# Attention scores in stages of three head pairs instead of two, the third in the two projection banks

## The chip, the cores and the metric

The kernel runs on one core of one Trainium2 chip. The metric is the device time of one execution in microseconds; less is better. Every tensor is fp32.

## The reference

A decoder layer on x (4 batches, 1024 tokens, 512 features) with a context of 384 features per token. Three residual blocks follow each other:

```
x = x + attn(layernorm(x))          # 16 heads of 32; gated
x = x + xattn(layernorm(x), ctx)    # 16 heads of 32; keys and values from ctx
x = x + ffn(layernorm(x))           # 64 small networks of 16 hidden units

attn:  s = softmax(q k^T / sqrt(32)) * aperture * expression, divided by its row sum + 1e-8
       out = rotate(s v) @ Wout
xattn: out = softmax(q k^T / sqrt(32)) v @ Wo + bo
```

What matters here is the inner part of both attentions: for each batch, head and 1024 x 1024 pair of tokens a score, its exponential, the sum of exponentials over the keys, and the product with the values.

## The kernel before

The work is eight units: `ph` 0 (attn) for batches 0 to 3, then `ph` 1 (xattn) for batches 0 to 3. Each unit has two halves `hf` of 512 queries. A half has four groups `g` of four heads (HG = 4), and each group eight key tiles `kt` of 128 keys. One (g, kt) is a **step**; there are 8 x 2 x 4 x 8 = 512.

In a step, `scores(g, kt)` (L600) makes two **pairs**, i = 0 and 1, each of two heads. A pair gets a tile `s` of two PSUM banks (pool `ps`, two such tiles, L71). For each of its heads j, two matmuls of 32 rows x 64 columns fill the bank (L607 to L611): the head's 32 features lie on partitions (2i+j) x 32 onward, so that pair 0 uses array rows 0 to 63 and pair 1 rows 64 to 127. One ScalarE instruction exponentiates both banks into a tile `e` (L613; pool `p4`, six buffers, L612). VectorE adds the exponentials up over kt into `es` (L619, L621), for both pairs or for pair 0 alone where pair 1's sums are made on TensorE (`shared`, which is phase 0 and the last unit); in phase 0 it also adds them up weighted by a gate, `eg` (L629).

`times` (L632) multiplies a step's exponentials with the values: four column matmuls of 128 rows x 32 columns into the accumulator `av` (L635), and in shared units, every second step, four more into `sm` (L643). `step` (L718) puts them one step late: scores of step n, then `times` of step n-1. After the last key tile `normalize` (L649) has ScalarE copy `av` and `sm` away; `add_up` (L662) and `divide` (L686) come steps later through `after` (L346) and its `tick`, and move the sums through DRAM on the SP queue.

PSUM has eight banks: four for `s`, two for `bank()` (pool `pf`, L72, L80), one each for `av` and `sm`. `bank()` serves everything else: the projections of the next unit (q, k, v), the output projections, transposes and the feed-forward.

The projections are made by `columns` (L83), four column matmuls per chunk of the contraction. Each of a projection's three or four chunks is one part with its own load (`proj` L445, `values` L514, `project` L787). `run` (L967) issues a half's 32 steps and, after each, as many parts of the side work (`beside`, L1001) as fit the share of the load that is due. So a projection is cut between steps, at one to three chunks a step. After a projection's last chunk its bank is copied to SBUF (`evacuate` L277, on ScalarE once the first unit has begun; on VectorE for the values of phase 0, L537).

In this way TensorE's queue in a half reads: scores of a step, `av` of the step before, perhaps `sm`, one to three projection chunks, then the next scores. The order of every engine is the program's own; no scheduler changes it.

Of the kernel before, what the change touches and what calls it, by code (L numbers as in the profile page):

```python
# [10 lines left out]
F32 = mybir.dt.float32  # L11
# [52 lines left out]
def moderate_path(tc: tile.TileContext, a: dict, out: bass.AP, flag: bass.AP):  # L64
    nc = tc.nc
    x = a["x"]
    with ExitStack() as st:
# [9 lines left out]
        p3 = enter(tc.tile_pool(name="mp3", bufs=3))  # L77
        p4 = enter(tc.tile_pool(name="mp4", bufs=4))

        def bank():  # L80
            return pf.tile([P, HALF], F32, tag="f", name="f")

        def columns(to, lhsT, rhs, **flags):  # L83

# [272 lines left out]
        def pre(u):  # L357
# [87 lines left out]
            def proj(what, g, hf):  # L445
                kind = "ctx" if ph == 1 and what == "k" else "in"
                n = NCK if kind == "ctx" else NC

                def part(cs):
                    def f():  # L450
                        if cs[0] == 0:
                            if "w" + what not in me:
                                fetch(what)
                            me["pj"] = bank()
                        for c in cs:
# [58 lines left out]
            def values(kt):  # L514
# [5 lines left out]
                def part(cs):  # L520
                    def f():
                        if cs[0] == 0:
                            if kt == 0:
                                if "wv" not in me:
                                    fetch("v")
                                me["v"] = p2.tile([P, NT, H, DH], F32, tag="v", name="v")
                            me["pv"] = bank()
                        for c in cs:
# [56 lines left out]
        def attention(u, hf):  # L585
# [11 lines left out]
            def closing(g):  # L597
                return (u, hf, g) == (len(order) - 1, 1, HG - 1)

            def scores(g, kt):  # L600
                q, k = me["q", hf], me["k"]
                es = []
                for i in range(2):
                    s = ps.tile([P, 2, HALF], F32, tag="s", name="s")
                    for j in range(2):
                        r = slice((2 * i + j) * DH, (2 * i + j + 1) * DH)
                        for m in range(0, P, 64):  # L607
                            nc.tensor.matmul(  # L608
                                s[m : m + 64, j, :], lhsT=k[r, g, kt * P + m : kt * P + m + 64], rhs=q[r, g, :],
                                start=True, stop=True,  # L610
                            )  # L611
                    e = p4.tile([P, 2, HALF], F32, tag="e", name="e", bufs=6)  # L612
                    nc.scalar.activation(e, s, AF.Exp, scale=SCALE)  # L613
                    es.append(e)
                me["e", kt] = es
                for i in range(1 if shared and not closing(g) else 2):
                    if kt == 1:
                        me.setdefault("es", {})[i] = p1.tile([P, 2, HALF], F32, tag=f"es{i}", name="es")
                        nc.vector.tensor_tensor(me["es"][i], me["e", 0][i], es[i], ALU.add)  # L619
                    elif kt > 1:  # L620
                        nc.vector.tensor_tensor(me["es"][i], me["es"][i], es[i], ALU.add)  # L621
                if ph == 0 and kt > 0:
                    if kt == 1:
                        me["eg"] = p1.tile([P, 2, HALF], F32, tag="es1", name="eg")
                    for h in range(2):
                        eg, gate = me["eg"][:, h, :], lambda t: me["sw"][:, t, HG * g + h, 1:2]
                        if kt == 1:
                            nc.vector.tensor_scalar(eg, me["e", 0][0][:, h, :], gate(0), None, ALU.mult)
                        nc.vector.scalar_tensor_tensor(eg, es[0][:, h, :], gate(kt), eg, ALU.mult, ALU.add)  # L629
                return es  # L630

            def times(g, kt, es):  # L632
                for h in range(HG):
# [5 lines left out]
                if shared and kt % 2 and not closing(g):  # L639

                    for j in range(4):
                        t, h = kt - 1 + j // 2, j % 2
                        nc.tensor.matmul(  # L643
                            sm[j * DH : j * DH + sums, :],
                            lhsT=me["sw"][:, t, HG * g + 2 + h, :] if ph == 0 else ones, rhs=me["e", t][1][:, h, :],
                            start=(kt == 1), stop=(kt == NT - 1),
                        )

            def normalize(g):  # L649
                i = (u * 2 + hf) * HG + g  # L650
                both = p1.tile([P, 3, HALF], F32, tag="both", name="both")
                nc.scalar.copy(both[:, 0, :], av)
                if shared:
                    nc.scalar.copy(both[:, 1, :], sm)
                    added = [me["es"][0][:, 0, :], me["es"][0][:, 1, :]]
                    if ph == 0:
                        added += [me["eg"][:, 0, :], me["eg"][:, 1, :]]
                else:
                    added = [me["es"][h // 2][:, h % 2, :] for h in range(HG)]
                after(1, lambda: add_up(g, i, both, added), behind=True)  # L660

            def add_up(g, i, both, added):  # L662
# [52 lines left out]
                nc.vector.tensor_tensor(me["q", hf][:, g, :], both[:, 0, :], all_, ALU.mult)  # L715
                me["divided", hf] = g

            def step(g, kt):  # L718
                def f():
                    issue_due(False)  # L720
                    es = scores(g, kt)
                    issue_due(True)
                    if late:
                        late.pop(0)()
                    late.append(lambda: finish(g, kt, es))
                    tick[0] += 1
                return f

            def finish(g, kt, es):
                times(g, kt, es)  # L730
                if kt == NT - 1 and not closing(g):
                    normalize(g)

            for g in range(HG):
                for kt in range(NT):
                    steps.append(step(g, kt))
            return steps

        def settle(u, hf, g):

# [4 lines left out]
            def sums():  # L745
                for j in range(HG):
                    nc.tensor.matmul(
                        sm[j * DH : (j + 1) * DH, :], lhsT=ones.to_broadcast([P, DH]), rhs=me["es"][j // 2][:, j % 2, :],
                        start=True, stop=True,
                    )  # L750

# [10 lines left out]
        def post(u, hf):  # L762
# [24 lines left out]
            def project(t):  # L787
                def part(cs, to=None):
                    def f():
                        assert last or me["divided", hf] >= cs[-1]  # L790
                        if cs[0] == 0:
                            res["po"] = to() if to else bank()
                            res["po", t] = res["po"]
                        if last:
                            res["po"] = res["po", t]
                        for c in cs:
# [167 lines left out]
                done = upto  # L964
            return [out + second[done:]]

        def run(main, items):  # L967

            parts = sum(items, [])
            total = sum(c for c, _ in parts)  # L970
            done = 0
            for n, f in enumerate(main):
                f()
                while parts and (done + parts[0][0] / 2 <= total * (n + 1) / len(main) or n == len(main) - 1):
# [26 lines left out]
        def beside(u, hf):  # L1001
# [77 lines left out]
        run([lambda: None], first)  # L1079
# [7 lines left out]
        late.pop(0)()  # L1087

        def go(*parts):
            for _, f in parts:  # L1090
# [673 lines left out]
```

## Time and profile before

| | |
|---|---|
| median of three runs | 2196.32 us (2192.43 to 2196.33) |
| profiled execution | 2195.77 us |
| its span | 2193.9 us, 53076 instructions |
| TensorE's granted clock, mean | 0.997 |
| L87, all projections: largest row (f<-xT,w) | 333.7 us busy, 2816 records, 592 ns |
| L621, es additions on VectorE | 642.4 us busy, 534 of 1227 ns |
| L629, eg additions on VectorE | 318.4 us busy, 448 of 746 ns |
| L652, L654, L666, copies of av and sm on ScalarE | 37.3, 23.9 and 37.4 us busy, 591 to 613 ns |
| mean DMA rate | 74 GB/s |

How to read it: PE is TensorE's matmuls, PEld its weight loads, which run beside them. DVE is VectorE, ACT ScalarE, POOL GpSimd, SP the engine whose queue issues most transfers. A group's line gives the line of code, engine, operation, out<-in with shapes, the count, busy time and mean duration in ns, then the engine's idle time before the group and what ended it. Ends of matmuls are modelled, and a matmul's 592 ns overlap with the next ones; what TensorE really spends is read from the distance between starts. An fp32 matmul leaves two records.

### The profile page before, as it was taken

To read this page: it belongs to the slowest core of one execution; us is meant where nothing else is said; L and a number is where in the kernel's file an instruction comes from. 1 tells how busy PE (TensorE), PEld (TensorE's weight loads), DVE (VectorE), ACT (ScalarE), POOL (GpSimd) and SP (SyncE) were. 2 spreads that over 40 slices of the span, in tenths; PEclk is the share of its full clock that TensorE was granted. 3 is DMA by queue.
4 is the path that set the end of the run, shared out by engine and by line. 5 is a ranking of instruction groups with operands and counts; after the bars stand their busy time and mean duration, and the time that the engine had idled before them with its cause. 6 is when DMAs were issued, how large, how long until landed. Compare 5 with 4: busy or idle time off the path is not lost.

```text
span 2193.9 us, 53076 instructions
## 1 busy us (share of the span) xinstructions
PE 2168.4 (99%) x22750; PEld 557.5 (25%) x22750; DVE 1558.3 (71%) x2510; ACT 1240.3 (57%) x1493; POOL 85.3 (4%) x127
## 2 busy tenths in 40 slices
PE   9999999999999999999999999999999999999996
PEld 4322222222222222222222222222222222222223
DVE  4578675796757957577686676877777777856477
ACT  0155545555455554555656566675757666577673
POOL 2000000030300000000000000000000000000000
PEclk9999999999999999999999999999999999999998
DMA  6312133032330221211222132221223142203131
GB/s 170 117 47 72 56 97 105 19 89 66 101 113 19 85 66 51 84 37 42 69 85 94 41 93 65 79 82 48 68 89 108 50 103 69 81 20 85 54 89 41
DMA packets 154137, 161.72 MB, mean 74 GB/s; under 512 B 47002, under 2 KB 92698, under 8 KB 152740
## 3 DMA queue, kind: packets, MB, share of 16 engines
q1 hardware_dynamic: 149828, 156.14, 24.7%
q8 instruction: 180, 2.95, 0.6%
q0 software_dynamic: 2080, 0.98, 0.3%
q10 hardware_dynamic: 1984, 1.12, 0.2%
q14 instruction: 65, 0.53, 0.1%
HBM read 115.40 MB, written 42.74 MB: 72 GB/s over the span
## 4 chain that ended last, share of the span: by engine, by line
PE 94%; DVE 2%; ACT 1%; issue 1%; DMA 1%; SPq 0%; POOL 0%; DVEq 0%; ACTq 0%
PE f L87 36%; PE s L608 25%; PE av L635 21%; PE sm L643 6%; PE sm L665 3%; ACT e L613 1%; DVE es L621 1%; PE f L913 1%; PE f L875 1%; PE s L87 1%; DVE g L902 1%; DMA xin<-in_x 0%; PE f L483 0%; PE s L913 0%; ACT hid L896 0%
## 5 line engine op out<-in xcount | busy, mean ns | idle before, releaser
L613 ACT ACTIVATE e<-s 128x1024 f32<-128x1024 f32 x1024 | 993.7, 1022 | 709.5 <-PE s L608 511.9
L621 DVE TENSOR_TENSOR es<-es,e 128x1024 f32<-128x1024 f32 x534 | 642.4, 1227 | 266.0 <-ACT e L613 264.2
L608 PE MATMUL s<-q,k 32*64 32x512 f32 x8192 | 607.3, 613 | 2.4 <-ACT e L613 0.8
L635 PE MATMUL av<-e,v 128*32 128x512 f32 x4096 | 550.2, 603 | 0.0
L87 PE MATMUL f<-xT,w 128*32 128x512 f32 x2816 | 333.7, 592 | 0.0
L629 DVE SCALAR_TENSOR_TENSOR eg<-e,sw,eg 128x512 f32<-128x512 f32 x448 | 318.4, 746 | 2.3
L619 DVE TENSOR_TENSOR es<-e 128x1024 f32<-128x1024 f32 x89 | 106.7, 1223 | 220.3 <-ACT e L613 188.4
L608 PEld LDWEIGHTS s<-q,k 32*64 32x64 f32 x8192 | 132.8, 129 | 446.2 <-ACT e L613 241.8
L87 PE MATMUL f<-w,q 128*32 128x512 f32 x1984 | 240.3, 592 | 0.0
L635 PEld LDWEIGHTS av<-e,v 128*32 128x32 f32 x4096 | 87.9, 108 | 403.9 <-issue 401.3
L87 PEld LDWEIGHTS f<-xT,w 128*32 128x32 f32 x2816 | 92.1, 110 | 210.5 <-issue 206.0
L643 PE MATMUL sm<-e,sw 128*2 128x512 f32 x1024 | 133.3, 592 | 0.0
L87 PE MATMUL f<-w,xT 128*32 128x512 f32 x896 | 106.0, 592 | 0.6 <-DVE q L285 0.6
L87 PEld LDWEIGHTS f<-w,q 128*32 128x32 f32 x1984 | 65.5, 110 | 149.1 <-issue 142.6
L87 PE MATMUL f<-w,ctxT 128*32 128x512 f32 x768 | 92.6, 592 | 0.0
L896 ACT ACTIVATE hid<-sT,units 128x256 f32<-128x256 f32 x128 | 76.5, 605 | 28.5 <-DVE g L902 24.1
L87 PE MATMUL f<-ctxT,w 128*32 128x512 f32 x768 | 92.3, 592 | 0.0
L812 POOL TENSOR_TENSOR r<-res,bo_bc 128x512 f32<-128x512 f32 x32 | 40.9, 1278 | 1041.5 <-DVE res L804 790.9
L902 DVE SCALAR_TENSOR_TENSOR g<-hid,units,g 128x256 f32<-128x256 f32 x120 | 57.5, 479 | 14.2 <-ACT hid L896 9.1
L665 PE MATMUL sm<-es,fixed 128*1 128x512 f32 x348 | 65.0, 591 | 0.0
L804 DVE TENSOR_TENSOR res<-f,res 128x512 f32<-128x512 f32 x62 | 42.5, 685 | 14.9 <-PE f L87 11.1
L715 DVE TENSOR_TENSOR q<-both,recb 128x512 f32<-128x512 f32 x63 | 43.2, 685 | 7.0 <-DMA recb<-rec_d 7.0
(265 smaller groups left out, 1046.2 us busy)
## 6 DMA issues: line engine op xcount, KB each, us to landing
recb<-rec_d SPq DMA_DIRECT2D x252, 64.0 KB
xT<-rows_d SPq DMA_DIRECT2D x60, 256.0 KB
rows_d<-r SPq DMA_DIRECT2D x60, 256.0 KB
w<-in_xattn_Wo SPq DMA_DIRECT2D x9, 1024.0 KB
w<-wout_d SPq DMA_DIRECT2D x8, 1024.0 KB
res<-in_x SPq DMA_DIRECT2D x32, 256.0 KB
x1b_d<-r SPq DMA_DIRECT2D x32, 256.0 KB
res<-x1b_d SPq DMA_DIRECT2D x32, 256.0 KB
```

The source lines that it names most:

```text
L87: nc.tensor.matmul(to[r], lhsT=lhsT[:, j, :] if len(lhsT.shape) == 3 else lhsT[:, r], rhs=rhs, **flags)
L608: nc.tensor.matmul(s[m : m + 64, j, :], lhsT=k[r, g, kt * P + m : kt * P + m + 64], rhs=q[r, g, :], start=True, stop=True,)
L613: nc.scalar.activation(e, s, AF.Exp, scale=SCALE)
L619: nc.vector.tensor_tensor(me["es"][i], me["e", 0][i], es[i], ALU.add)
L621: nc.vector.tensor_tensor(me["es"][i], me["es"][i], es[i], ALU.add)
L629: nc.vector.scalar_tensor_tensor(eg, es[0][:, h, :], gate(kt), eg, ALU.mult, ALU.add)
L635: nc.tensor.matmul(av[r, :], lhsT=me["v"][:, kt, HG * g + h, :], rhs=es[h // 2][:, h % 2, :], start=(kt == 0), stop=(kt == NT - 1),)
L643: nc.tensor.matmul(sm[j * DH : j * DH + sums, :], lhsT=me["sw"][:, t, HG * g + 2 + h, :] if ph == 0 else ones, rhs=me["e", t][1][:, h, :], ...
L665: nc.tensor.matmul(sm[j * DH : j * DH + 1, :], lhsT=ones, rhs=e, start=True, stop=True)
L715: nc.vector.tensor_tensor(me["q", hf][:, g, :], both[:, 0, :], all_, ALU.mult)
L896: nc.scalar.activation(hid, res["s"], AF.Relu, bias=units[:, 1, h : h + 1], scale=units[:, 0, h : h + 1])
L902: nc.vector.scalar_tensor_tensor(res["g"], res["hid"], units[:, 2, h - 1 : h], res["g"], ALU.mult, ALU.add)
```

## The change

A half's 64 pairs (g, kt, i) are now listed in order, and a **phase** takes three at a time instead of a step taking two; the last of a half takes the one that is left. If a projection is open in a bank at that moment (`open_`, counted by `keep`), it takes two. The first two pairs of a phase get `s` tiles, the third two tiles of `bank()`. The third pair's exponentials are two ScalarE instructions of 512 columns, one for each bank. Where a projection is due right after and the phase has three pairs (`front`), the pairs are multiplied in the order 1, 2, 0, so that pair 0 lies in the banks; ScalarE still takes them in the order 0, 1, 2 and so empties the banks first.

`times` of the steps that the phase before completed come after the phase's scores; one or two steps, since three pairs complete one step and a half. Where a group ends (`border`), the first of them, which ends the group, comes after the first exponential, and the other after the side work of the phase. `tick` now advances by 1.5.

`run_phases` takes the place of `run`: it issues side work after a phase's scores, and does not stop while a projection is open, so that each projection is issued whole. A projection is due by its first chunk's place in the load.

`e`, `es` and `eg` now share one tag with eight buffers (`wide`); before, `e` had six, and `es` and `eg` buffers of their own. In the last unit a pause in the side work is 14 or 12 instead of 10.

```diff
+        def keep(first, last):
+            open_[0] += bool(first) - bool(last)
...
+            def multiply_into(g, kt, i, two):
                 q, k = me["q", hf], me["k"]
-                    s = ps.tile([P, 2, HALF], F32, tag="s", name="s")
-                    e = p4.tile([P, 2, HALF], F32, tag="e", name="e", bufs=6)
-                    nc.scalar.activation(e, s, AF.Exp, scale=SCALE)
+                for j in range(2):
+                    r = slice((2 * i + j) * DH, (2 * i + j + 1) * DH)
+                    for m in range(0, P, 64):
+                        nc.tensor.matmul(
+                            two[j][m : m + 64], lhsT=k[r, g, kt * P + m : kt * P + m + 64], rhs=q[r, g, :],
+                            start=True, stop=True,
+                        )
+
+            def wide():
+                return p4.tile([P, 2, HALF], F32, tag="e", name="e", bufs=8)
+
+            def exponentials(g, kt, i, two, whole):
+                e = wide()
+                if whole is not None:
+                    nc.scalar.activation(e, whole, AF.Exp, scale=SCALE)
+                else:
                     for j in range(2):
+                        nc.scalar.activation(e[:, j, :], two[j], AF.Exp, scale=SCALE)
+                me.setdefault(("e", g, kt), {})[i] = e
...
-            def step(g, kt):
-                def f():
-                    issue_due(False)
-                    es = scores(g, kt)
-                    issue_due(True)
-                    if late:
-                        late.pop(0)()
-                    late.append(lambda: finish(g, kt, es))
-                    tick[0] += 1
-                return f
...
+            pairs = [(g, kt, i) for g in range(HG) for kt in range(NT) for i in range(2)]
+
+            def phase(size, early):
+
+                issue_due(False)
+                mine, pairs[:] = pairs[:size], pairs[size:]
+                front = early and size == 3
+                order_ = [1, 2, 0] if front else range(len(mine))
+                places = {}
+                for n, j in enumerate(order_):
+                    whole = ps.tile([P, 2, HALF], F32, tag="s", name="s") if n < 2 else None
+                    two = [bank(), bank()] if whole is None else [whole[:, m, :] for m in range(2)]
+                    multiply_into(*mine[j], two)
+                    places[j] = (two, whole)
+                border = len(late) > 1 and late[0][0] == NT - 1
+                for n, pair in enumerate(mine):
+                    exponentials(*pair, *places[n])
+                    add(*pair)
+                    if n == 0 and border:
+                        issue_due(True)
+                        late.pop(0)[1]()
+                issue_due(True)
+                while late and not border:
+                    late.pop(0)[1]()
+                now = list(late)
+                late.clear()
+                for g, kt, i in mine:
+                    if i == 1:
+                        late.append((kt, lambda g=g, kt=kt: finish(g, kt, me["e", g, kt])))
+                tick[0] += size / 2
+                return lambda: [f() for _, f in now]
...
+        def run_phases(pairs, phase, items):
...
+            while pairs:
+                size = min(len(pairs), 2 if open_[0] else 3)
+                upto = total * (all_ - len(pairs) + size) / all_
...
+                others = phase(size, early)
+                while parts and (open_[0] or due(parts[0][0], done)):
                     c, f1 = parts.pop(0)
                     if f1:
                         f1()
                     done += c
+                others()
...
-                out += pause(2) + weave(h[0:k], pause(10)) + weave(h[k:], last["o"]) + held.pop()["out"]
+                out += pause(2) + weave(h[0:k], pause(14 if hf else 12)) + weave(h[k:], last["o"]) + held.pop()["out"]
...
-                run(attention(u, hf), beside(u, hf))
+                run_phases(*attention(u, hf), beside(u, hf))
```

More of the change, by code (lines that the diff above doesn't have):

```diff
@@ L78, in moderate_path @@
         p4 = enter(tc.tile_pool(name="mp4", bufs=4))
+        open_ = [0]
         def bank():
             return pf.tile([P, HALF], F32, tag="f", name="f")
+        def keep(first, last):
+            open_[0] += bool(first) - bool(last)
         def columns(to, lhsT, rhs, **flags):
@@ L454, in f @@
                             me["pj"] = bank()
+                        keep(cs[0] == 0, cs[-1] == n - 1)
                         for c in cs:
@@ L527, in f @@
                             me["pv"] = bank()
+                        keep(cs[0] == 0, cs[-1] == n - 1)
                         for c in cs:
@@ L598, in closing @@
                 return (u, hf, g) == (len(order) - 1, 1, HG - 1)
-            def scores(g, kt):
+            def multiply_into(g, kt, i, two):
                 q, k = me["q", hf], me["k"]
-                es = []
-                for i in range(2):
-                    s = ps.tile([P, 2, HALF], F32, tag="s", name="s")
-                    for j in range(2):
[L606 to L611, printed above, removed]
-                    e = p4.tile([P, 2, HALF], F32, tag="e", name="e", bufs=6)
[L613 to L616, printed above, removed]
-                    if kt == 1:
[L618 to L622, printed above, removed]
@@ new lines, in add @@
+            def add(g, kt, i):
+                if kt == 0:
+                    return
+                e0, e = me["e", g, 0], me["e", g, kt]
+                if i == 0 or not shared or closing(g):
+                    if kt == 1:
+                        me.setdefault(("es", g), {})[i] = wide()
+                        nc.vector.tensor_tensor(me["es", g][i], e0[i], e[i], ALU.add)
+                    else:
+                        nc.vector.tensor_tensor(me["es", g][i], me["es", g][i], e[i], ALU.add)
+                if ph == 0 and i == 0:
@@ L623, in scores @@
                     if kt == 1:
-                        me["eg"] = p1.tile([P, 2, HALF], F32, tag="es1", name="eg")
+                        me["eg", g] = wide()
                     for h in range(2):
-                        eg, gate = me["eg"][:, h, :], lambda t: me["sw"][:, t, HG * g + h, 1:2]
+                        eg, gate = me["eg", g][:, h, :], lambda t: me["sw"][:, t, HG * g + h, 1:2]
                         if kt == 1:
-                            nc.vector.tensor_scalar(eg, me["e", 0][0][:, h, :], gate(0), None, ALU.mult)
@@ L629, in scores @@
-                        nc.vector.scalar_tensor_tensor(eg, es[0][:, h, :], gate(kt), eg, ALU.mult, ALU.add)
-                return es
+                            nc.vector.tensor_scalar(eg, e0[0][:, h, :], gate(0), None, ALU.mult)
+                        nc.vector.scalar_tensor_tensor(eg, e[0][:, h, :], gate(kt), eg, ALU.mult, ALU.add)
             def times(g, kt, es):
@@ L644, in times @@
                             sm[j * DH : j * DH + sums, :],
-                            lhsT=me["sw"][:, t, HG * g + 2 + h, :] if ph == 0 else ones, rhs=me["e", t][1][:, h, :],
+                            lhsT=me["sw"][:, t, HG * g + 2 + h, :] if ph == 0 else ones, rhs=me["e", g, t][1][:, h, :],
                             start=(kt == 1), stop=(kt == NT - 1),
@@ L654, in normalize @@
                     nc.scalar.copy(both[:, 1, :], sm)
-                    added = [me["es"][0][:, 0, :], me["es"][0][:, 1, :]]
+                    added = [me["es", g][0][:, 0, :], me["es", g][0][:, 1, :]]
                     if ph == 0:
-                        added += [me["eg"][:, 0, :], me["eg"][:, 1, :]]
+                        added += [me["eg", g][:, 0, :], me["eg", g][:, 1, :]]
                 else:
-                    added = [me["es"][h // 2][:, h % 2, :] for h in range(HG)]
+                    added = [me["es", g][h // 2][:, h % 2, :] for h in range(HG)]
                 after(1, lambda: add_up(g, i, both, added), behind=True)
@@ L732, in finish @@
                     normalize(g)
[L734 to L737, printed above, removed]
+            pairs = [(g, kt, i) for g in range(HG) for kt in range(NT) for i in range(2)]
[27 more added lines that the diff above has]
+                return lambda: [f() for _, f in now]
+            return pairs, phase
         def settle(u, hf, g):
@@ L747, in sums @@
                     nc.tensor.matmul(
-                        sm[j * DH : (j + 1) * DH, :], lhsT=ones.to_broadcast([P, DH]), rhs=me["es"][j // 2][:, j % 2, :],
+                        sm[j * DH : (j + 1) * DH, :], lhsT=ones.to_broadcast([P, DH]), rhs=me["es", g][j // 2][:, j % 2, :],
                         start=True, stop=True,
@@ L793, in f @@
                             res["po", t] = res["po"]
+                        keep(cs[0] == 0, cs[-1] == NC - 1)
                         if last:
@@ L965, in weave, with run, due @@
             return [out + second[done:]]
-        def run(main, items):
+        def run(items):
+            for _, f1 in sum(items, []):
+                if f1:
+                    f1()
+        def run_phases(pairs, phase, items):
             parts = sum(items, [])
-            total = sum(c for c, _ in parts)
+            total, all_ = sum(c for c, _ in parts), len(pairs)
             done = 0
-            for n, f in enumerate(main):
-                f()
-                while parts and (done + parts[0][0] / 2 <= total * (n + 1) / len(main) or n == len(main) - 1):
+            while pairs:
+                size = min(len(pairs), 2 if open_[0] else 3)
+                upto = total * (all_ - len(pairs) + size) / all_
+                def due(c, at):
+                    return at + min(c, 1) * 2 <= upto or len(pairs) == 0
+                early, at = False, done
+                for c, f1 in parts:
+                    if early or not due(c, at):
+                        break
+                    early, at = bool(c and f1), at + c
+                others = phase(size, early)
+                while parts and (open_[0] or due(parts[0][0], done)):
                     c, f1 = parts.pop(0)
@@ L1078, in moderate_path @@
         first += p["v"][1][0:3] + pres[1]["tr"][0] + p["v"][1][3:]
-        run([lambda: None], first)
+        run(first)
         for u in range(n):
@@ L1083, in moderate_path @@
             for hf in range(2):
-                run(attention(u, hf), beside(u, hf))
+                run_phases(*attention(u, hf), beside(u, hf))
         tail = ending[0]
         sums, divide, look = settle(n - 1, 1, HG - 1)
-        late.pop(0)()
+        late.pop(0)[1]()
         def go(*parts):
```

## The prediction

> **What bounds the kernel now.** I read the page's totals first, then its slices and the chain that ended last, then the costliest groups, and last the order of time around two score stages.
>
> ```profile
> PE 2168.4 (99%) x22750; PEld 557.5 (25%) x22750; DVE 1558.3 (71%) x2510; ACT 1240.3 (57%) x1493; POOL 85.3 (4%) x127
> ...
> PEclk9999999999999999999999999999999999999998
> ...
> PE 94%; DVE 2%; ACT 1%; issue 1%; DMA 1%; SPq 0%; POOL 0%; DVEq 0%; ACTq 0%
> PE f L87 36%; PE s L608 25%; PE av L635 21%; PE sm L643 6%; PE sm L665 3%; ACT e L613 1%; DVE es L621 1%; PE f L913 1%; PE f L875 1%; PE s L87 1%; DVE g L902 1%; DMA xin<-in_x 0%; PE f L483 0%; PE s L913 0%; ACT hid L896 0%
> ```
>
> TensorE is the bound: busy 99%, at the full granted clock, and 94% of the chain. So a change pays only where it takes time out of TensorE's own queue, and it costs whatever it puts in. A quarter of the chain is the scores of L608, the very thing that is regrouped.
>
> ```profile
> L613 ACT ACTIVATE e<-s 128x1024 f32<-128x1024 f32 x1024 | 993.7, 1022 | 709.5 <-PE s L608 511.9
> ...
> L608 PE MATMUL s<-q,k 32*64 32x512 f32 x8192 | 607.3, 613 | 2.4 <-ACT e L613 0.8
> L635 PE MATMUL av<-e,v 128*32 128x512 f32 x4096 | 550.2, 603 | 0.0
> ```
>
> A score matmul uses 32 rows and 64 columns of the array, the other work 128 rows and 32 columns; a matmul leaves two records, one for each fp32 pass. TensorE's idle time does not show as idle, because ends are modelled; so I read starts. First an ordinary stage of two pairs, TensorE alone:
>
> ```profile
> 802.58 0.61 PE L87 MATMUL f<-xT,w 128*32 128x512 f32 x4
> 803.12 1.11 PE L608 MATMUL s<-q,k 32*64 32x512 f32 x16
> 804.16 0.64 PE L635 MATMUL av<-e,v 128*32 128x512 f32 x4
> ```
>
> The stage takes 1.04 us from its first matmul to the next work's. Its 16 records start in two bursts of eight, 0.48 us apart: both pairs run side by side. Elsewhere one pass of four column matmuls follows the last after 0.43 us; into the stage it is 0.54, and the first pass after it takes 0.45. Now a stage whose second pair came late:
>
> ```profile
> 101.63 0.21 PEld L608 LDWEIGHTS s<-q,k 32*64 32x64 f32 x8 [1.03 <-ACT e L613]
> 101.63 2.00 PE L608 MATMUL s<-q,k 32*64 32x512 f32 x16
> 102.55 0.21 PEld L608 LDWEIGHTS s<-q,k 32*64 32x64 f32 x8 [0.71 <-ACT e L613]
> 102.79 1.94 ACT L613 ACTIVATE e<-s 128x1024 f32<-128x1024 f32 x2 [0.29 <-PE s L608]
> 103.56 0.16 PEld L635 LDWEIGHTS av<-e,v 128*32 128x32 f32 x8 [0.81 <-issue]
> 103.56 1.06 PE L635 MATMUL av<-e,v 128*32 128x512 f32 x8
> ```
>
> The two pairs run one behind the other, at 101.63 and 102.55, and the stage takes 1.93 us: a pair that cannot lie beside another costs 0.89 us more. That is the row the forecast rests on.
>
> Over all 512 stages in the trace, from first score to next work: 435 take 1.04 to 1.08 us, 22 take 1.88 to 1.94, the rest lie between; the sum is 571.7 us, 37 us above 512 x 1.044. Those 37 us are nearly all that TensorE waits for ScalarE today.
>
> **The change, part by part.** It is done as said: in the built order of TensorE the 512 stages of eight score matmuls become 336 of twelve and 16 of four (each half unit has 64 pairs, 21 x 3 + 1). Nothing else on TensorE changes in number.
>
> *Fewer switches: a gain.* A switch costs 0.54 - 0.43 on entry and 0.45 - 0.43 after, together 0.137 us unrounded. There are 512 - 352 = 160 fewer: -21.9 us. What the stage itself loses at its ends is in its length, next.
>
> *A third pair in a stage: the cost.* A pair i uses array rows 64i to 64i+63 (heads 2i and 2i+1, the slice in L606). Pairs come in turn i = 0, 1, 0, then 1, 0, 1, so the third is always on the rows of one of the others, and its two passes must follow that one's two. The other half of the array stands empty meanwhile. Nearest row: the serial stage, 1.93 us, +0.89. From below: two bare passes, 2 x 0.429 = +0.86. From above: +0.89 and what it waits for its banks (below). I take the row. 336 x 1.932 + 16 x 1.044 = 665.8 us for 571.7: +94.2 us. This assumes that all 37 us of late second pairs go; if all stay, it is +131.
>
> Two rules of the Trainium skill bear on this. TensorEngine Tiling (Array Packing), section Tiling Modes, says that changing the tiling mode drains the engine; that speaks for fewer stages, and the rows price it: 0.137 us outside the stage and 1.044 - 0.858 = 0.186 inside. TensorE: Matmul & The Clock Gate, Part 3, gives a pack's span as one matmul plus about 4 ns for each further tile. By that alone twelve matmuls would cost about 1.06 us: 336 x 1.06 + 16.7 - 571.7 - 21.9 = -221 us. But it counts distinct tiles, and the first page's list has eight tiles in the 32x64 mode, all of which the two pairs already fill. The rows agree with eight (16 records in two bursts, a late pair at full price), so I use +0.89.
>
> *The third pair's PSUM.* It takes the two projection banks, and is written last, 0.91 us into the stage. After a whole projection one of these banks must first be evacuated: a 128x512 ScalarE copy is 0.59 us (L281's row), and in the trace it starts about 0.1 us after the last matmul; some 0.85 us into the stage it is done, just inside the cover of the first two pairs. If ScalarE is busy then, the third pair waits and with it av, sm and everything queued behind on TensorE. VectorE evacuates some values (L537), behind 1.23 us additions: up to 1 us each, for some 24 projections. Below nothing: no, because the bank had no such reader before.
>
> *Exponentials by halves.* Two 128x512 ones replace a wide one 336 times. Wide ones start 0.92 us apart (1.94 us for two); halves by the copy row 0.59 each, about 0.5 apart: +0.06 to +0.26 us x 336 = 20 to 90 us of ScalarE, which is 57% busy. TensorE's projections hide it where a phase has one. In phases without one ScalarE needs 2 x 0.92 + 1.0 = 2.9 us for the three pairs from 1.15 us into the stage (804.27 - 803.12 in the ordinary stage), so the banks come free at about 2.2, 3.1 and 4.1. The next stage starts at 1.93 + 0.86 + 0.13 = 2.9 us with four av matmuls, 3.8 with av and sm or two steps of av, 4.6 with both. From the built order: 35 phases of the first kind, 29 of the second, some 30 of the third. The second pair and the third (due 0.91 later) are late by 0.3 to 1.3 us in the first, about 0.4 in the second, not in the third: 35 x 0.5 + 29 x 0.4 = 29 us; between 10 and 60. I take 28.
>
> *e, es and eg in one pool of eight.* Before, six e plus their own es. Now es and eg hold two of eight, four where one g passes to the next. By the built order's waits an exponential then waits for av of the same phase, issued right after the scores; ScalarE stalls under the projection, at no cost where there is one. It is in the 10 to 60.
>
> *Projections whole, evacuations, ticks.* Same matmuls in the same mode: nothing. The delayed steps now come due in ticks of 1.5, so sums, the reciprocal and the product with q come up to one step later. Their SP queue transfers (rec_d, recb, sums) move with them, past the loads and rows_d there; the output projections that need q lie later still, and SP moves 74 GB/s on average. Nothing; if that cover is gone, one late q costs a few us once in a half unit. VectorE's work stays 71% and the same.
>
> Sum: -21.9 + 94.2 + 28 = +100 us. Span 2193.9 + 100 = 2294; the profiled execution took 2195.77, so 1.9 lie around the span: 2296. The median of the runs, 2196.32, is 0.5 above that execution, nothing beside the rest.
>
> **The rivals.**
>
> *No new waits.* Three pairs give ScalarE slack, and with bare passes the third pair costs 0.86: 94.2 - 10 - 21.9 = +62 us, 2258. For it: ScalarE is 57% busy. Against: its slack is not in the phases without projections. 0.12.
>
> *ScalarE and the e buffers become the bound in phases.* Each of some 100 phases without a projection, and the borders between g, lose 1 to 1.5 us: +72 + 100 or more, 2350. For it: 22 stages are already serial today, many in the last unit. Against: the average phase has 2294 / 352 = 6.5 us for 3.5 us of ScalarE. 0.10.
>
> *The other side: the third pair is not serial.* If its passes slip under the others' second pass, at one pass only, a stage is 1.47 us: 336 x 1.474 + 16.7 - 571.7 - 21.9 = -82 us, with waits 2140. It decides at the stage's length: below 1.71 us the change gains (571.7 + 21.9 - 16.7 = 576.9, over 336), before waits. Against it: the same tiles must stream 512 columns twice, 0.43 us a pass wherever it is seen. 0.03.
>
> **How the numbers follow.** Main case 0.75, time 2296; its own width is the waits of 10 to 60 us, 2278 to 2328. I reach to the first rival and a little above the main case: 2258 to 2335. Left out: most of the second rival, and the third. Slower 0.97, faster 0.02, within 0.2% 0.01; 0.2% (4 us) is about what a measurement can tell.
>
> **What would show it.** Right: 352 stages, ordinary ones of twelve taking 1.9 us or more, with a third burst 0.91 us after the first and a fourth; TensorE still 99% busy; the score line's share of the chain up from 25% to about 29%; ScalarE's wide exponentials down to 688. Wrong: twelve matmuls in under 1.7 us; or stages often over 2.3 us, with TensorE's wait for the exponentials as the long row; or TensorE well below 99%, which would make buffers or ScalarE the cause.

## The result, and the profile after

The changed kernel takes 2480.03 us (2471.74 to 2486.74, 4 runs) against 2195.37 us (4 runs of it, one more than in the table of before): ratio 1.130, 95% interval 1.126 to 1.134. The direction was right, and the size was not: 285 us more where 100 were forecast, and 145 us above the end of the range. The profiled execution, which the account below is made from, is the fastest of the four: 2471.74 us.

The page of the changed kernel, its totals, clock and chain:

```profile
span 2470.0 us, 53205 instructions
...
PE 2356.1 (95%) x22750; PEld 661.5 (27%) x22750; DVE 1560.7 (63%) x2510; ACT 1261.8 (51%) x1829; POOL 84.7 (3%) x127
...
PEclk9999999999999999999989999999999999999998
...
PE 57%; DVE 3%; ACT 3%; issue 1%; DMA 1%; SPq 0%; DVEq 0%; ACTq 0%
```

TensorE was 99% busy and 94% of the chain; now 95% and 57%. The forecast named this as a sign that it was wrong ("TensorE well below 99%, which would make buffers or ScalarE the cause"). The scores were to take about 29% of the chain, and take 19% (`s` and `f` of L612). The granted clock, 0.997 before, is 0.981 on average here and 0.974 to 0.980 in the other three runs. The groups of the page say who was waited for:

```profile
L623 ACT ACTIVATE e<-s 128x1024 f32<-128x1024 f32 x688 | 673.1, 1032 | 213.1 <-PE s L612 122.4
L626 ACT ACTIVATE e<-f 128x512 f32<-128x512 f32 x672 | 370.0, 599 | 532.7 <-PE f L612 400.2
...
L612 PE MATMUL f<-q,k 32*64 32x512 f32 x2688 | 417.3, 597 | 33.3 <-DVE v L544 10.1
...
L659 PE MATMUL sm<-e,sw 128*2 128x512 f32 x1024 | 135.5, 601 | 33.7 <-ACT both L682 33.7
```

The third pairs' matmuls (`f` of L612) wait for VectorE's copy of a projection, and the `sm` matmuls for ScalarE's copy of a finished group's sums. Neither group had such a wait before: the scores of L608 had 2.4 us in all, and the `sm` group none:

```profile
L643 PE MATMUL sm<-e,sw 128*2 128x512 f32 x1024 | 133.3, 592 | 0.0
```

First an ordinary stage of three pairs, TensorE alone, to see that the price of the third pair itself was right:

```profile
1719.92 0.61 PE L92 MATMUL f<-w,ctxT 128*32 128x512 f32 x4
1720.46 1.11 PE L612 MATMUL s<-q,k 32*64 32x512 f32 x16
1721.40 1.04 PE L612 MATMUL f<-q,k 32*64 32x512 f32 x8
1722.36 1.07 PE L651 MATMUL av<-e,v 128*32 128x512 f32 x8
```

The third pair starts 0.94 us in, and the stage takes 1.90 us; 203 of the 336 stages of three take 1.86 to 1.92. Now one stage with its surroundings, where the rest of the time is:

```profile
616.14 2.32 PE L612 MATMUL s<-q,k 32*64 32x512 f32 x16
...
618.28 1.02 PE L612 MATMUL f<-q,k 32*64 32x512 f32 x4
...
618.49 1.41 DVE L646 SCALAR_TENSOR_TENSOR e<-e,sw 128x512 f32<-128x512 f32 x2
619.82 0.54 DVE L309 TENSOR_SCALAR xin<-xin,bnmv,yi 128x512 f32<-128x512 f32 x1
620.27 0.69 DVE L544 TENSOR_TENSOR v<-f,sw 128x512 f32<-128x512 f32 x1
...
621.01 1.97 PE L612 MATMUL f<-q,k 32*64 32x512 f32 x4 [1.71 <-DVE v L544]
622.91 0.11 PEld L681 LDWEIGHTS sm<-e,fixed 128*1 128x1 f32 x8 [1.61 <-issue]
622.91 1.89 PE L681 MATMUL sm<-e,fixed 128*1 128x512 f32 x8
...
624.83 1.08 ACT L626 ACTIVATE e<-f 128x512 f32<-128x512 f32 x2 [7.51 <-PE sm L681]
625.80 1.95 ACT L623 ACTIVATE e<-s 128x1024 f32<-128x1024 f32 x2
...
627.61 0.62 ACT L682 COPY both<-sm 128x512 f32<-128x512 f32 x1
...
628.28 1.04 PE L659 MATMUL sm<-e,sw 128*2 128x512 f32 x8 [1.78 <-ACT both L682]
```

Three things follow each other. The third pair's first head starts at 618.28. The second head's bank still holds a value projection that ended before 616.14; VectorE gets to it at 620.27, behind its additions and a layernorm step, so the head starts at 621.01, 2.7 us after the first, where in the ordinary stage above both start together. Then the four `sm` matmuls of L681 (eight records) take 1.89 us where 1.04 is usual. Last, the sums' copy L682 stands behind ScalarE's four exponentials, and `sm` and all behind it wait for it until 628.28. Why the matmuls slowed down, a table of stretches of the same trace shows (in a row, the length and five pairs of busy time and count are followed by the granted clock, the DMA share and the GB/s):

```profile
613.44:620.27 6.83, 5.72 (x48) 1.34 (x40) 4.30 (x7) 1.11 (x2) 0.00 (x0) 1.00 0.00 1
620.27:627.10 6.83, 5.49 (x20) 0.79 (x20) 0.92 (x3) 2.27 (x4) 0.00 (x0) 0.50 0.20 77
```

The clock is halved for 6.83 us, from 620.27, in the middle of the wait. Between 100 us and the last score there are 17 such stretches, 75 us together, and TensorE is busy in 68 of these 75 us. If it did half its work in them, some 34 us were lost; that is an estimate. Before had no such stretch there.

The account of the two profiled executions, from the starts of TensorE's records (excess over the usual distance of the same two kinds of work):

| term | forecast | measured |
|---|---|---|
| score stages without waits: 336 x 1.90 + 16 x 1.02 for 571.7 us | +94.2 | +83.0 |
| 160 switches fewer | -21.9 | -21.9, since the distances at a stage's two ends are the same (0.54 and 0.45 us in both traces) |
| waits inside the score stages (791.4 us in all) | +28 | +136.7 |
| the remainder: sm behind the sums' copy 40, the rest spread out | 0 | +78 |
| sum | +100 | +276 |

The 34 us of half clock are inside the last two measured terms: of the 68 us, 18 lie inside score stages and 50 outside, which makes some 9 and 25 us by the same estimate. By what the program makes each delayed matmul wait for, about 67 us of the waits inside stages are for VectorE's evacuations (res, v, the feed-forward's outputs, w), 28 for ScalarE's, 33 for exponentials. Which wait ended last is inferred, so these three are good to a few us.

### The profile page after: what moved, and what is told of

Its sections match the earlier page's. It is cut to its first block, busy times and chain, and to the rows that moved or that the text cites. A ratio compares the mean times of both kernels' runs of the same rounds, so it can differ in the third digit from the quotient of the medians.

```text
span 2470.0 us, 53205 instructions
## 1 busy us (share of the span) xinstructions
PE 2356.1 (95%) x22750; PEld 661.5 (27%) x22750; DVE 1560.7 (63%) x2510; ACT 1261.8 (51%) x1829; POOL 84.7 (3%) x127
## 4 chain that ended last, share of the span: by engine, by line
PE 57%; DVE 3%; ACT 3%; issue 1%; DMA 1%; SPq 0%; DVEq 0%; ACTq 0%
PE f L92 19%; PE av L651 13%; PE s L612 10%; PE f L612 9%; PE sm L659 3%; PE sm L681 2%; ACT e L623 2%; PE f L910 1%; DVE e L638 1%; PE f L948 1%; DVE g L937 0%; ACT e L626 0%; DMA rec_d<-rec 0%; DVE res L954 0%; DMA res<-in_x 0%
## 5 line engine op out<-in xcount | busy, mean ns | idle before, releaser
L638 DVE TENSOR_TENSOR e<-e 128x1024 f32<-128x1024 f32 x534 | 638.7, 1224 | 452.3 <-ACT e L623 255.2
L623 ACT ACTIVATE e<-s 128x1024 f32<-128x1024 f32 x688 | 673.1, 1032 | 213.1 <-PE s L612 122.4
L626 ACT ACTIVATE e<-f 128x512 f32<-128x512 f32 x672 | 370.0, 599 | 532.7 <-PE f L612 400.2
L612 PE MATMUL f<-q,k 32*64 32x512 f32 x2688 | 417.3, 597 | 33.3 <-DVE v L544 10.1
L612 PE MATMUL s<-q,k 32*64 32x512 f32 x5504 | 419.9, 617 | 3.1 <-ACT e L623 1.4
L646 DVE SCALAR_TENSOR_TENSOR e<-e,sw 128x512 f32<-128x512 f32 x448 | 318.3, 746 | 2.3
L636 DVE TENSOR_TENSOR e<-e 128x1024 f32<-128x1024 f32 x89 | 108.5, 1224 | 229.3 <-ACT e L623 142.5
L651 PEld LDWEIGHTS av<-e,v 128*32 128x32 f32 x4096 | 104.9, 110 | 386.3 <-issue 370.1
L612 PEld LDWEIGHTS f<-q,k 32*64 32x64 f32 x2688 | 128.5, 132 | 256.9 <-issue 119.7
L612 PEld LDWEIGHTS s<-q,k 32*64 32x64 f32 x5504 | 91.1, 131 | 311.5 <-issue 186.6
L839 DVE TENSOR_TENSOR res<-f,res 128x512 f32<-128x512 f32 x62 | 42.5, 686 | 72.2 <-PE f L92 49.7
L668 ACT COPY both<-av 128x512 f32<-128x512 f32 x63 | 37.4, 594 | 92.7 <-issue 28.6
```

Source lines behind the costliest of these rows:

```text
L612: nc.tensor.matmul(two[j][m : m + 64], lhsT=k[r, g, kt * P + m : kt * P + m + 64], rhs=q[r, g, :], start=True, stop=True,)
L623: nc.scalar.activation(e, whole, AF.Exp, scale=SCALE)
L626: nc.scalar.activation(e[:, j, :], two[j], AF.Exp, scale=SCALE)
L636: nc.vector.tensor_tensor(me["es", g][i], e0[i], e[i], ALU.add)
L638: nc.vector.tensor_tensor(me["es", g][i], me["es", g][i], e[i], ALU.add)
L646: nc.vector.scalar_tensor_tensor(eg, e[0][:, h, :], gate(kt), eg, ALU.mult, ALU.add)
```

## The experiments

All times are medians, with before run on the same chip beside them. Edits are to the changed kernel unless said otherwise. My first theory, A: the third pair costs two serial passes, and the rest is waits for its banks and for the sums' copy. Rival B: whole projections and the shared e buffers are at fault, whoever holds the banks.

**Two pairs a phase, projections whole.**

```diff
-                size = min(len(pairs), 2 if open_[0] else 3)
+                size = min(len(pairs), 2)
```

> The changed kernel with two pairs a phase again; projections stay whole, and e, es and eg share eight buffers. Theory A (the third pair costs two further passes a stage, and its two banks are waited for behind the evacuation of the projection): no score stage waits for a bank, stages are 1.04 us again, the time is within 30 us of before, 2185 to 2225. Rival B (whole projections and the shared e buffers starve ScalarE and VectorE, whoever holds the banks): most of the 285 us stays, above 2380.

2321.5 us, ratio 1.056 (1.055 to 1.058). Both theories missed: A by 100 us, B by 60. Taking the third pair away takes away only 158 us of the 285; 126 us stay without it. The trace of this run, two steps without side work:

```profile
1500.02 2.00 PE L612 MATMUL s<-q,k 32*64 32x512 f32 x16
1500.93 0.21 PEld L612 LDWEIGHTS s<-q,k 32*64 32x64 f32 x8 [0.71 <-ACT e L623]
1501.18 1.94 ACT L623 ACTIVATE e<-s 128x1024 f32<-128x1024 f32 x2 [0.29 <-PE s L612]
1501.95 1.07 PE L651 MATMUL av<-e,v 128*32 128x512 f32 x8
1502.95 0.43 PEld L612 LDWEIGHTS s<-q,k 32*64 32x64 f32 x16 [0.84 <-ACT e L623]
1502.95 1.31 PE L612 MATMUL s<-q,k 32*64 32x512 f32 x16
```

The second pair waits for the exponential that empties its banks (0.71 us, ACT e L623), and the stage becomes the serial one of 1.93 us. Such stages of 1.9 us are 119 of 512 here, 22 before; the sum of the stages is 674 us for 572. A projection issued whole leaves other steps bare, and a bare step is shorter on TensorE than ScalarE's two exponentials and the way there and back. This became theory C.

**The sums' copy early.** L682 is issued after the phase's first exponential:

```diff
-                    if n == 0 and border:
+                    if n == 0:
                         issue_due(True)
+                    if n == 0 and border:
                         late.pop(0)[1]()
```

> The changed kernel, but the single-row sums of a finished group and ScalarE's copy of them are issued after the first exponential of a phase, not after the third. Theory A: the wait of the sm matmuls for that copy (20 waits, 40 us in the trace) goes, and with it some windows of half clock: 40 to 60 us faster, 2420 to 2440. Rival B: the wait only moves to the next exponential's e tile, within 15 us of the changed kernel.

2426.4 us, ratio 1.106 (1.104 to 1.108): 54 us less than the changed kernel. The excess before `sm` falls from 40 to 9 us, as A expected. The half-clock stretches fall from 17 to 12, but last 75 us together as in the changed kernel.

**The additions late.** VectorE's es and eg additions follow the side work, so that they no longer stand ahead of a projection's evacuation:

```diff
                     exponentials(*pair, *places[n])
-                    add(*pair)
...
-                return lambda: [f() for _, f in now]
+                return lambda: [add(*pair) for pair in mine] + [f() for _, f in now]
```

> The changed kernel, but the additions of a phase (es and eg on VectorE) are issued after the phase's side work, so that a bank's evacuation on VectorE no longer stands behind them. Theory A: the third pair's waits for VectorE's evacuations (v, res, outputs; 67 us of 130 in the score stages) go, with some half-clock windows: 60 to 90 us faster, 2390 to 2420. Rival B: e tiles are held longer, so it is slower than the changed kernel.

2416.9 us, ratio 1.101 (1.099 to 1.102): 63 us less. The stages sum to 731 us for 791. The size is as A expected, the way to it only in part: read in the same manner from both traces, the stages' waits for VectorE's evacuations fall from some 64 to 37 us and do not go; those for ScalarE's evacuations fall from 28 to 4, and those for exponentials from 33 to 24. Why ScalarE's evacuations come sooner with the additions late is open.

**Both edits.**

> Both edits together, early sums and late additions. Theory A: the two gains add up, 2330 to 2380, mean granted clock back to 0.99; the floor is the serial third pair, before plus 62 to 72 us = 2257 to 2267, and no version with three pairs gets under before. Rival B: above 2440.

2377.0 us, ratio 1.082 (1.081 to 1.084): 103 us less, most of the two gains added. The clock came back to 0.985 only, where 0.99 was expected. The evacuations of `res` still make three long waits, 17 us together, the longest of 10. The changed kernel has the same wait:

```profile
1263.63 1.11 PE L612 MATMUL s<-q,k 32*64 32x512 f32 x16
1264.05 1.91 SPq L813 DMA_DIRECT2D res<-in_x  x4
...
1270.92 0.69 DVE L839 TENSOR_TENSOR res<-f,res 128x512 f32<-128x512 f32 x1 [12.26 <-DMA res<-in_x]
...
1271.67 1.97 PE L612 MATMUL f<-q,k 32*64 32x512 f32 x4 [6.11 <-DVE res L839]
```

The load of the residual that L839 adds is issued only at 1264.05, by SP's queue, behind the sums, xT and w, after the projection that needs it has been multiplied; VectorE waits 12.3 us for it, and the third pair, which needs that projection's bank, waits with it. In before's trace no residual addition waits for its load.

**Two pairs, side work by chunks again,** with the buffers, ticks and pauses of the change:

```diff
-                size = min(len(pairs), 2 if open_[0] else 3)
+                size = min(len(pairs), 2)
...
-                while parts and (open_[0] or due(parts[0][0], done)):
+                while parts and (done + parts[0][0] / 2 <= upto or not pairs):
```

> As the run with two pairs a phase and whole projections, but the side work is cut by chunks again, as before. Theory C (revised: whole projections leave steps without side work, in which the two exponentials of ScalarE take longer than TensorE's scores and av, and the next second pair comes late; the third pair's cost is on top): back to before, 2188 to 2206. Rival B' (the shared eight buffers and the ticks cost the 125 us, wholeness does not): stays at 2300 to 2330.

2208.7 us, ratio 1.0055 (1.0041 to 1.0069). Wholeness is 113 of the 126 us; the edit also brings back before's rule of when a part is due, and the two were not run apart. 13 us remain, 3 more than C allowed.

**The same with the last unit's pauses at 10.**

```diff
-                out += pause(2) + weave(h[0:k], pause(14 if hf else 12)) + weave(h[k:], last["o"]) + held.pop()["out"]
+                out += pause(2) + weave(h[0:k], pause(10)) + weave(h[k:], last["o"]) + held.pop()["out"]
```

> Two pairs a phase, side work by chunks, and the pauses of the last unit at 10 as before; what stays of the change is the order of the code, the ticks and the eight shared buffers. Theory C: the 13 us above before lie in the last unit and come of the longer pauses, so it is back at before, within 6 us, 2190 to 2202. Rival: the shared buffers cost them, it stays at 2205 to 2212.

2195.0 us, ratio 0.9996 (0.9987 to 1.0004): before again. The 13 us are the longer pauses of the last unit; the shared buffers of e, es and eg and the ticks cost nothing by themselves with two pairs a phase.

**The same with the pauses of the change and the sums' copy early** (the edit of sums_early on the two-pair kernel with chunks).

> Two pairs a phase, side work by chunks, and the sums of a finished group with ScalarE's copy of them issued after the first exponential of the step instead of the second. Theory C: before has no wait of sm for that copy, so nothing is to be had, within 8 us of the run without this edit, or a little slower since the second exponential and with it the next second pair come 0.6 us later in 63 steps. Rival: the late copy costs there too, 15 to 40 us faster, below 2180, and a version that beats both kernels.

2211.5 us, ratio 1.0067 (1.0054 to 1.0081), 3 us more than without it. No version that beats before came of it.

**The third pair's matmuls twice.** Disputed cost, measured by itself:

```diff
                     multiply_into(*mine[j], two)
+                    if n == 2:
+                        multiply_into(*mine[j], two)
```

> The changed kernel with the third pair's score matmuls issued twice, into the same banks with the same values (work added, result the same). Theory A (two passes of 0.429 us that nothing else of the stage can overlap): 336 x 0.858 = 288 us more than the changed kernel, 2750 to 2785. Rival (a third pair lies beside other work of the stage, or its cost is mostly the wait for its banks): under 150 us more, below 2630.

2776.1 us, ratio 1.262 (1.259 to 1.265): 296 us more than the changed kernel, where two passes 336 times are 288. TensorE alone in this run:

```profile
1732.13 1.11 PE L612 MATMUL s<-q,k 32*64 32x512 f32 x16
1733.04 1.91 PE L612 MATMUL f<-q,k 32*64 32x512 f32 x16
1734.87 1.93 PE L651 MATMUL av<-e,v 128*32 128x512 f32 x16
```

The stage takes 2.74 us for 1.90: 0.84 to 0.86 more. A pair on rows that are taken hides behind nothing. That the totals agree within 8 us is partly luck, since half-clock stretches grew from 75 to 164 us as well. The length of the stage is the evidence.

**Two pairs, whole projections, half of the exponentials left out.** ScalarE exponentiates 256 of 512 columns and GpSimd writes ones into the rest:

```diff
-                    nc.scalar.activation(e, whole, AF.Exp, scale=SCALE)
+                    nc.gpsimd.memset(e[:, :, 256:], 1.0)
+                    nc.scalar.activation(e[:, :, 0:256], whole[:, :, 0:256], AF.Exp, scale=SCALE)
...
```

> Two pairs a phase and whole projections, but ScalarE exponentiates only 256 of each head's 512 columns; GpSimd fills the rest of e with ones (part of the softmax is left out). TensorE's work is the same. Theory C (in steps without side work ScalarE's exponentials set the pace): most of the 113 us of whole projections goes, 2200 to 2240. Rival (VectorE's additions or the evacuations set it): over 2290.

2229.6 us, ratio 1.015 (1.014 to 1.017). 92 us go, with TensorE's work unchanged; stages of 1.9 us fall from 119 to 2. Of the 34 us that stay, 13 are the pauses, and 21 are not accounted for. So theory C holds for most of it: whole projections cost what ScalarE cannot keep up with in bare steps.

**The changed kernel with the same edit, on the halves of the third pair too.**

> The changed kernel with the same half of the exponentials left out on ScalarE and filled with ones by GpSimd. Theory A (the waits of the third pair are mostly for banks that VectorE evacuates behind its additions, and those start earlier only by what the exponentials are shorter): part goes, 2350 to 2420; the sm wait for the copy behind the exponentials shrinks by half, 20 us. Rival (ScalarE's exponentials are all of it): down to the floor of the serial third pair, 2265 to 2300. Second rival (evacuations alone): above 2440.

2416.3 us, ratio 1.099 (1.097 to 1.102): 64 us less, at the upper end of A's range. Lighter exponentials let the sums' copy and the additions start earlier, and leave most.

**Both edits and half of the exponentials.**

> Early sums and late additions together, and half of each exponential left out on ScalarE and filled with ones by GpSimd (part of the softmax is left out). Theory A: another 40 to 70 us below the 2377 of the two edits, 2305 to 2340, still 40 or more above the floor of the serial third pair, because some evacuations still stand in VectorE's queue. Rival (ScalarE was all that was left): the floor, 2257 to 2275.

2349.5 us, ratio 1.072 (1.070 to 1.074). 28 us less than both edits alone, not 40 to 70: A's size was off. Evacuations in VectorE's queue still take 40 us of waits.

**And half of VectorE's additions left out.** `es` and `eg` are summed over 256 columns, the rest is filled by GpSimd:

```diff
-                        nc.vector.tensor_tensor(me["es", g][i], me["es", g][i], e[i], ALU.add)
+                        nc.vector.tensor_tensor(me["es", g][i][:, :, 0:256], me["es", g][i][:, :, 0:256], e[i][:, :, 0:256], ALU.add)
...
```

> As the run before this one, and VectorE's additions es and eg also over 256 of 512 columns, the rest filled with constants by GpSimd (more of the softmax sums is left out). TensorE's work is that of the changed kernel. Theory A: near the floor that the serial third pair sets with no waits, 2257 to 2300, and not below 2250: three pairs a stage lose even where nothing is waited for. Rival (the third pair itself is cheap and the loss is all waits): below 2230.

2300.0 us, ratio 1.049 (1.047 to 1.050), at the upper end of what was expected. The stages sum to 685.6 us, 31 above 654.7 without waits; a third of these is one wait of 10 us for a residual. Less the 31, the 6 before `sm` and the 13 of the pauses (if they cost here what they cost with two pairs), 2250 remain, some 55 us above before, where bare stages and switches come to 83.0 - 21.9 = 61. Three pairs a stage lose where almost nothing is waited for.

## Why the prediction was wrong, point by point

- **What bounds the kernel:** right. TensorE's queue was the bound, and all 285 us were put into it.
- **The third pair's passes, +0.89 us:** right. A stage takes 1.90 us where 1.93 was taken: the recorded lower bound, two bare passes or +0.86, is what a pair costs. Doubling the passes adds 0.84 to 0.86 us a stage again. The third rival, the third pair not being serial, falls with it, and so does the 1.06 us of one pack. The term came to +83.0 for +94.2.
- **"The third pair's PSUM": the failed step.** The 28 us of waits in the sum were worked out from late exponentials alone (35 x 0.5 + 29 x 0.4, which make 29), and the waits for exponentials came to about 33: that part held. For evacuations the text allowed "up to 1 us each" for some 24 projections on VectorE and called ScalarE's "just inside the cover of the first two pairs", but the sum has nothing for either. Measured: about 67 us for VectorE's and 28 for ScalarE's. It missed the additions of residuals to the output projections (L839) and to the feed-forward's outputs (L954), which hold a bank and stand on VectorE, too; my reading gives them more than half of the 67. And an evacuation comes only after what is queued ahead of it, which made the third pair's second head 2.7 us late in the stage shown. Taking VectorE's additions from ahead of everything gave 63 us back, under half of it at VectorE's evacuations.
- **"Projections whole, evacuations, ticks": "Same matmuls in the same mode: nothing".** Wrong. Whole projections alone cost 113 us with two pairs. I had seen the phases without side work, but charged the third pair with them; the point is that cutting a projection into chunks is what kept every step long enough for ScalarE. In the changed kernel part of this is paid in another form, since three pairs wait less for exponentials (33 us), so 113 and the terms of the account do not add up. The loads were not all covered either: I allowed a few us for a late q, and leaned on 74 GB/s that the page gives for all queues together; one late `res` alone made a stage 8 us longer (10 with both edits).
- **The sums' copy:** not in the forecast. L682 moved behind three pairs' exponentials, where before it stood behind two, with `sm` of the same phase queued behind it: 40 us in the account, 54 us in the run.
- **The clock:** not in the forecast. Half-clock stretches, most of them in or after waits, cost an estimated 34 us.
- **Exponentials by halves:** right. ScalarE spends 1043.1 us on exponentials for 993.7, 49 more, where 20 to 90 were forecast.
- **The pause edit:** not costed; 13 us in the two-pair kernel.
- **e, es and eg in one pool:** right that it costs nothing by itself, as far as the two-pair kernel shows.
- **The rivals:** the second (2350, phases losing 1 to 1.5 us) was nearer in time, but its engine was ScalarE and the buffers, and lighter exponentials took back 64 us alone. Its own terms, 72 and 100 or more on top of 2196, make 2368 or more and not 2350. Over all, 215 us of waits and slow stretches stand against the 28 in the sum.

What stays open: of the 78 us outside the stages, 40 stand before `sm` and some 25 are half clock by the estimate above; the rest was not traced to single waits. Three pairs with projections in chunks can't be had in this layout, since the third pair needs both banks, and this was not tried.

## What to carry to other kernels

Count the tiles of the array that a stage fills before putting more into it: a further piece on rows that are taken costs its full passes, whatever switch it saves. Lending a buffer to the busiest engine makes every other user's evacuation part of that engine's path, so price each by the whole queue ahead of it and by the loads it needs. And side work in small pieces between steps is what hides a slower engine; gathered into blocks it leaves bare steps, at that engine's pace.

## What the runs showed of the hardware

TensorE's granted clock fell to half for 3.4 to 10.2 us at a time, 17 times in the changed kernel, and the stretches begin on a grid of 3.41 us. The 3.41 us ahead of a drop held 0.8 to 3.2 us without a matmul in progress, but other such stretches with up to 1.9 us were followed by none. Waits are not the whole trigger: in the run with both edits the clock also fell at 757.93, after 3.41 us in which the profile has TensorE busy throughout, nearly all of it with one stage of three pairs. No threshold can be read from this, and what sets the drops off is not shown. Part 1 of TensorE: Matmul & The Clock Gate, in the Trainium skill, gives as its rule that TensorE should have no idle gaps over some 3.4 us; here shorter ones came ahead of most drops. The same part tells of a kernel whose clock swung from frequent short idle times, which is nearer to this case.
